# A two-layer graph attention kernel: one aggregate of layer 0 divided once more, its left sums made in the two aggregates in front

## The chip, the cores and the metric

The kernel runs on one core of a Trainium2 chip. The metric is the device time in microseconds of one execution. The kernel before was timed three times: 3044.36, 3051.23 and 3053.49 us, median 3051.23 us.

Engines are named as in the profile: PE is TensorE (PEld its weight loads), DVE is VectorE, ACT is ScalarE, POOL is GpSimd, SP is the engine that issues most loads.

## The reference

Two attention layers over 2708 nodes with 1024 features each. In both, every node attends to its neighbours in `adj`; the kernel spends its time in float32 products of 1024- and 2708-sized matrices.

```python
# layer 0
h = jnp.maximum(_layernorm(x), 0.0)
f = h @ Wf + bf;  g = h @ Wg + bg
e = relu(f @ g.T)
attention = softmax(where(adj > 0, e, NEG), axis=1)
x = x + attention @ (h @ W + bW)
# layer 1
h = jnp.maximum(_layernorm(x), 0.0)
hw = h @ W1
e = leaky_relu(hw @ a1 + (hw @ a2).T, 0.2)
attention = softmax(where(adj > 0, e, NEG), axis=1)
x = x + relu(attention @ hw)
```

The kernel multiplies by W after the attention: `(attention @ h) @ W`. The product `attention @ h`, before its multiplication by W, is called the aggregate here.

## The kernel before

**Tiling.** Rows of the attention (the nodes that look) come in five panels of 576, 576, 532, 512 and 512. The nodes that are looked at come in twenty tiles of 128, as ten pairs (`NQ`, a "pair" is also called q), with a small rest in two more tiles, MONO and TINY, called the left-over. The exponentials of one panel stay in on-chip memory: two tiles for each pair, plus two for the left-over.

**Products with seven instead of eight multiplications.** Every large product is split in 2 x 2 blocks and computed by Winograd's variant of Strassen's method with the seven products M1 to M7. Some operands are blocks as they are, some are sums and differences of blocks. The sums of the left side are made once and kept in HBM; those of the right side (the exponentials) are made on VectorE in place.

- In layer 0 the left side of the aggregate is `hg_d`, five tensors, each for two pairs, with the seven operands of 512 columns. `rows_h` writes the four that are blocks, `sums_h` reads them back, makes the other three and overwrites M5.
- `aggregate` (line 914) computes one panel's aggregate with `accumulate` (line 657). A product is 10 pairs x 4 blocks of 128 output rows, 40 matmuls, whose moving side is half a panel wide: 256 columns in panels 3 and 4. The order is M1, M5, M2, M6, M3, M7, M4. The results are collected in the temporary tiles m1, m15, u2 and in the result tile `gT`.
- In layer 1 the same is done for panel 0. In panels 1 to 4 `aggregate_quartered` (line 1085) is used: each of the seven products is split once more in the same way. A product is then seven inner products of 5 x 2 matmuls with a quarter of a panel as moving side, 128 columns in panels 3 and 4. `quarters_of` (line 1028) makes the inner sums of the right side in tiles named `quarter`, five for each product, four sums in each. `put_quarters` makes those of the left side (tiles `hq`) from `hr_d` and stores them in `hs2_d`. An inner product loads one tile `hc2`; two tiles `hl2` per product hold the last part of it.

**Order of work.** All loads on SP run in the program's order. Work that isn't urgent is put in lists of items, each with an assumed cost in us: `later` and `lazy`. After groups of matmuls the program calls `behind(us)`, which gives so much credit and runs items while credit is left; `lazy` is only used when `later` is empty and `spare[0]` is set, which in layer 0 is during the aggregates of panels 1 to 4. Before an item runs, the loads of the first `ahead[0]` items of its list are issued. `accumulate` calls `behind(rate)` four times in each product, with a rate of 3.0 in layer 0's aggregates; `aggregate_quartered` calls `behind(fine)` after each inner product. Beyond this, instructions without a fixed order are placed by a scheduler when the program is built, by when their inputs and buffers should be free.

**Around the change.** For every panel p layer 0 runs scores, the q-projection of the next panel (in which the softmax steps of this panel begin), the aggregate, and then, for panels 0 to 2, the projection by W. Panel 3's projection comes after the scores of panel 4, so the aggregate of panel 3 lies between a q-projection and scores. Layer 1's left sums `put_quarters` enter `lazy` as soon as four tiles of layer 0's result are known.

**Buffers.** `slot` has 54 buffers for panel-wide tiles, `stream` (tag "strm") 12 buffers of 4 KB per partition for tiles that are loaded and used once.

Of the kernel before, what the change touches and what calls it, by code (L numbers as in the profile page):

```python
# [8 lines left out]
FP = mybir.dt.float32  # L9
# [9 lines left out]
P = 128  # L19
W = 512  # L20
# [37 lines left out]
def kernel(  # L58
# [94 lines left out]
    hs_d = [dram.tile([P, 8, NH, P], FP, name=f"hs_d{q}") for q in range(NQ)]  # L153
    groups = [[q, q + 1] for q in range(0, NQ, 2)]
    group_of = {q: (i, j) for i, g in enumerate(groups) for j, q in enumerate(g)}
    assert sorted(group_of) == list(range(NQ))
    hg_d = [dram.tile([P, 7, len(g), W], FP, name=f"hg_d{i}") for i, g in enumerate(groups)]
    NK = NQ // 2
    WH = W // 2
    hr_d = dram.tile([P, 7, 2, 2, NK, WH], FP, name="hr_d")  # L160
    hs2_d = dram.tile([P, 7, 4, NK, WH], FP, name="hs2_d")

# [205 lines left out]
    def rows_h(q, ha, hb):  # L368

        i, j = group_of[q]  # L370
        for m, h in ((M1, ha[0]), (M5, ha[1]), (M2, hb[0]), (M4, hb[1])):
            store(hg_d[i][:, m, j], h)

    summed, sums_may = [0], [True]

    def sums_h():

        def fetch(q, two):
            i, j = group_of[q]
            for m in (M1, M2):  # L380
                two.append(stream("hr", (P, 2, W)))
                (load if "m" in got else by_scalar)(two[-1], hg_d[i][:, m:m + 2, j])

        def first(q, two):
            (a0, a1), (b0, b1) = ((t[:, 0], t[:, 1]) for t in two)
            add(b1, a1, b1)
            sub(a1, a0, a1)

        def second(q, two):
            (a0, a1), (b0, b1) = ((t[:, 0], t[:, 1]) for t in two)  # L390
            sub(a0, b1, a0)
            sub(b0, b0, a0)
            i, j = group_of[q]
            store(hg_d[i][:, M6:M7 + 1, j], two[0])
            store(hg_d[i][:, M3, j], b0)
            store(hg_d[i][:, M5, j], b1)
            summed[0] += 1
        for q in range(NQ):
            two = []
            put(1.4, lambda q=q, two=two: held(first, q, two), lambda q=q, two=two: fetch(q, two), ready=lambda: sums_may[0])  # L400
            put(1.4, lambda q=q, two=two: held(second, q, two), ready=lambda: sums_may[0])

    BY_QUARTERS = (M1, M5, M2, M6, M7, M3, M4)
    made_quarters = {}

    def put_quarters(m, k, to=lazy):

        two = []

        def fetch():  # L410
            if from_slots[0]:
                two.extend(slot(f"hq{h}", (P, 2, WH)) for h in range(2))
            else:
                t = stream("hq", (P, 4, WH))
                two.extend(t[:, 2 * h:2 * h + 2] for h in range(2))
            for h in range(2):
                nc.gpsimd.dma_start(two[h], hr_d[:, m, h, :, k])

        def go():
# [5 lines left out]
            for h in range(2):  # L425
                store(hs2_d[:, m, 2 * h:2 * h + 2, k], two[h])
            made_quarters[m] = made_quarters.get(m, 0) + 1
        put(1.7, go, fetch, to=to)

    def quarters_until(m):  # L430
        while made_quarters.get(m, 0) < NK:
            one(lazy if lazy else later)
# [491 lines left out]
    def aggregate(l, p, S, sm, then={}, rate=3.0):  # L924
# [28 lines left out]
        order_of_products = (M1, M2, M4, M5, M6, M3, M7) if first else (M1, M5, M2, M6, M3, M7, M4)  # L953
        steps = [(m, i) for m in order_of_products for i in range(len(groups))]

        def left(m, q, d):
            i, j = group_of[q]
            at = steps.index((m, i))
            for m_, i_ in steps[at:at + (3 if l else 1)]:
                if (m_, i_) not in hc:  # L960
                    hc[m_, i_] = stream("hc", (P, 4, WH) if l else (P, 2, W))
                    load(hc[m_, i_], hr_d[:, m_, :, :, i_].rearrange("p h f c -> p (h f) c") if l else hg_d[i_][:, m_])
            return hc[m, i][:, d // 2 * 2 + j, d % 2 * P:(d % 2 + 1) * P] if l else hc[m, i][:, j, d * P:(d + 1) * P]
# [70 lines left out]
    def quarters_of(p, S):  # L1034
# [47 lines left out]
        def fourth():  # L1082
            for q in range(NQ):
                sub(t1(q), wb_(q)[:, lo], wa_(q)[:, lo])
        return {"make": make, "right": right, "first": first, "fifth": fifth, "second": second, "fourth": fourth}

    def aggregate_quartered(p, S, sm, of_right, then={}, fine=1.2):

# [11 lines left out]
        def product(m, n, ps, start):  # L1100
            quarters_until(m)
            if (m, 0) not in lasts:
                for i, of in enumerate((hr_d[:, m, :, :, NK - 1].rearrange("p h f c -> p (h f) c"), hs2_d[:, m, :, NK - 1])):
                    lasts[m, i] = stream("hl2", (P, 4, WH))
                    load(lasts[m, i], of)
            t = stream("hc2", (P, NK - 1, WH))
            raw = n in (M1, M2, M4)
            i = {M1: 0, M2: 1, M4: 3, M6: 0, M3: 1, M7: 2, M5: 3}[n]
            load(t, hr_d[:, m, i // 2, i % 2, :NK - 1] if raw else hs2_d[:, m, i, :NK - 1])
            last = lasts[m, int(not raw)][:, i]  # L1110
# [10 lines left out]
        def left_over(banks, e, s, fresh):  # L1121

            two = stream("hl", (P, W + 2 * P))
            load(two, hgl_d[1][:, e])
            cols = lambda b: slice(s.start + b * hb, s.start + (b + 1) * hb)
# [43 lines left out]
        def with_second():  # L1169
# [3 lines left out]
        before_next = {M1: lambda: make(M5), M5: with_second, M2: lambda: (of_right["fourth"](), make(M6)), M6: lambda: make(M7),  # L1173
                       M7: lambda: make(M3), M3: lambda: make(M4)}
        left_out = None
        for m in BY_QUARTERS:
            V = [quad(*direct[m])[:, 2 * r:2 * r + 2] for r in range(2)] if m in direct else [v[:, :, :h] for v in in_pairs("V")]
            c11, c12 = (V[0][:, :, b * hb:(b + 1) * hb] for b in range(2))
# [39 lines left out]
            if m == M5:  # L1218
                of_right["second"]()
            if m == M5:  # L1220
                inverse.append(inverse_sums(p, sm))
            if m in then:
# [356 lines left out]
    def rows_done(t, xt):  # L1579
# [14 lines left out]
        if panel_of[t] == NP - 1:  # L1594
# [18 lines left out]
            else:  # L1613
# [16 lines left out]
                if q == NQ - 1:  # L1630
                    for m in BY_QUARTERS:
                        put_quarters(m, q // 2, later)
                    for p in range(2, NP):
# [16 lines left out]
        elif whole:  # L1650
# [3 lines left out]
            if quads_met[q // 2] == 2:  # L1654
                put(0.0, lambda: [put_quarters(m, q // 2) for m in BY_QUARTERS])

# [10 lines left out]

    ORDERED = (NP - 1,)

    def by_gpsimd(o, i, **k):  # L1670
# [97 lines left out]
    for p in range(NP):  # L1768
# [20 lines left out]
        spare[0], from_slots[0] = p > 0, p == NP - 1  # L1789
        G[p] = aggregate(0, p, S, got["sm"], then)  # L1790
        spare[0] = False
        if p == 0:
            flush()
            ahead[0] = 2
# [113 lines left out]
    for p in range(NP):  # L1908
# [5 lines left out]
        ahead[0] = 2 if p else 4  # L1914
        g = aggregate_quartered(p, S, sm, next_right, then, fine=1.0) if p else aggregate(1, p, S, sm, then, rate=4.0)
        hooks = {}
# [33 lines left out]
```

## Time and profile before

| | |
|---|---|
| three timed executions | 3044.36, 3051.23, 3053.49 us |
| the profiled execution | 3049.19 us |
| its span, first to last instruction | 3047.3 us |
| mean granted TensorE clock | 0.997 |
| HBM read / written | 630.04 MB / 138.11 MB |
| layer 0, aggregate of panel 1 | 838.8 to 987 us |
| layer 0, aggregate of panel 2 | 1235.8 to 1373 us |
| layer 0, aggregate of panel 3 | 1610.4 to 1742.4 us |
| layer 0, aggregate of panel 4 | 1926 to 2056.6 us |
| layer 1, aggregate of panel 3 (split) | 2698.3 to 2823.3 us |

How to read it: a busy share is a share of the span. A float32 matmul counts as two instructions on PE. Tile names in the trace are without their numbers, so `hs2_d` appears as `hs_d`, `hc2` as `hc` and `hl2` as `hl`; stages are told apart by their times. A chain of waits follows the work back from the last instruction, at each step to what released it.

### The profile page before, as it was taken

Reading aid. Unit: us, or ns where it says so; the run is one execution under the profiler, and the core shown is the slowest. Engines: PE = TensorE matmul, PEld = TensorE weight load, DVE = VectorE, ACT = ScalarE, POOL = GpSimd, SP = SyncE. Lnnn points to the kernel's source line nnn. Section 1 sums busy time; section 2 is a strip of 40 time slices with the busy share of each in tenths; the row PEclk is TensorE's granted clock in tenths of the full one; section 3 lists DMA queues with packets and bytes.
Section 4 is the critical chain, followed back from the end, with each engine's and each line's share of the span. In section 5 each row is a group of like instructions: output and inputs, shape, how many; then the busy total and the mean of one; then the engine's idle time right before and its main releaser. Section 6 shows DMA issues by size and latency. Waiting matters only on the chain.

```text
span 3047.3 us, 41722 instructions
## 1 busy us (share of the span) xinstructions
PE 2993.9 (98%) x14642; PEld 2294.2 (75%) x14642; DVE 2047.6 (67%) x4667; ACT 536.8 (18%) x880; POOL 496.9 (16%) x770
## 2 busy tenths in 40 slices
PE   8998999999999999999999999999999999999999
PEld 4576777667877588885888886784767959879695
DVE  5776794585742686616965276867878768887863
ACT  4420020020200121101210111302232121212200
POOL 1421111210112110223111111131212010020201
PEclk9999999999999999999999999999999999999999
DMA  6989878887466786768957588679768768878887
GB/s 232 302 271 272 311 276 308 264 286 235 133 236 165 228 273 195 247 156 251 292 188 251 179 241 258 223 292 335 245 212 264 263 202 299 294 265 297 264 294 268
DMA packets 392704, 766.78 MB, mean 252 GB/s; under 512 B 65728, under 2 KB 206944, under 8 KB 392464
## 3 DMA queue, kind: packets, MB, share of 16 engines
q1 hardware_dynamic: 332336, 584.80, 59.6%
q0 software_dynamic: 54464, 164.78, 16.1%
q10 hardware_dynamic: 5696, 14.55, 1.4%
q8 instruction: 116, 1.90, 0.2%
q14 instruction: 92, 0.75, 0.1%
HBM read 630.04 MB, written 138.11 MB: 252 GB/s over the span
## 4 chain that ended last, share of the span: by engine, by line
PE 73%; DVE 11%; issue 8%; DMA 5%; POOL 1%; ACT 1%; SPq 1%; POOLq 0%; DVEq 0%; ACTq 0%
PE sz L1425 6%; PE gy L679 6%; PE gz L679 6%; PE gz L1114 5%; PE gx L679 5%; PE sx L1425 4%; PE pz L1314 4%; PE sy L1425 4%; PE px L1314 4%; PE py L1314 3%; PE gy L1114 3%; PE gx L1114 3%; PE gv L679 3%; PE M_ps L591 3%; PE qz L679 2%
## 5 line engine op out<-in xcount | busy, mean ns | idle before, releaser
L1425 PE MATMUL sz<-B,As 128*128 128x288 f32 (+2 forms) x1200 | 292.0, 392 | 6.0 <-DVE st L45 5.1
L1425 PEld LDWEIGHTS sz<-B,As 128*128 128x128 f32 x1200 | 227.2, 190 | 55.2 <-DVE st L45 8.4
L1425 PE MATMUL sx<-B,As 128*128 128x288 f32 (+2 forms) x800 | 200.8, 394 | 12.4 <-DMA As<-hs_d 10.4
L1425 PE MATMUL sy<-B,As 128*128 128x288 f32 (+2 forms) x800 | 199.0, 392 | 0.0
L1425 PEld LDWEIGHTS sx<-B,As 128*128 128x128 f32 x800 | 152.5, 191 | 45.8 <-DMA As<-hs_d 9.5
L679 PE MATMUL gz<-Sa,hc 128*128 128x288 f32 (+2 forms) x800 | 185.8, 392 | 0.0
L679 PEld LDWEIGHTS gz<-Sa,hc 128*128 128x128 f32 x800 | 151.5, 190 | 32.2 <-issue 2.2
L1425 PEld LDWEIGHTS sy<-B,As 128*128 128x128 f32 x800 | 151.7, 190 | 30.6 <-DVE st L45 0.3
L1114 PE MATMUL gz<-quarter,hc 128*128 128x128 f32 (+2 forms) x1344 | 168.8, 279 | 3.8 <-DVE gT L45 3.7
L1114 PEld LDWEIGHTS gz<-quarter,hc 128*128 128x128 f32 x1344 | 160.6, 191 | 5.1 <-DVE gT L45 4.6
L143 POOL DMA_DIRECT2D out_dram<-x_res x164 | 81.2, 502 | 469.1 <-DVE x_res L45 461.9
L1314 PE MATMUL py<-w,ps 128*128 128x512 f32 x320 | 142.0, 593 | 0.0
L1314 PE MATMUL pz<-w,ps 128*128 128x512 f32 x320 | 142.0, 594 | 0.0
L1314 PE MATMUL px<-w,gT 128*128 128x512 f32 x320 | 141.1, 593 | 0.0
L679 PE MATMUL gy<-T,hc 128*128 128x288 f32 (+2 forms) x480 | 114.9, 402 | 3.8 <-DMA hc<-hg_d 3.8
L1314 PEld LDWEIGHTS pz<-w,ps 128*128 128x128 f32 x320 | 60.2, 190 | 76.2 <-issue 72.2
L1314 PEld LDWEIGHTS py<-w,ps 128*128 128x128 f32 x320 | 60.5, 190 | 75.1 <-issue 72.7
L591 PE MATMUL M_ps<-wgT,wfT 128*128 128x512 f32 x256 | 112.7, 596 | 1.6 <-ACT hsT L45 1.6
L1314 PEld LDWEIGHTS px<-w,gT 128*128 128x128 f32 x320 | 60.1, 190 | 71.3 <-issue 67.8
L679 PEld LDWEIGHTS gy<-T,hc 128*128 128x128 f32 x480 | 93.1, 194 | 24.7 <-DMA hc<-hg_d 4.3
L143 POOL DMA_DIRECT2D mk_d<-mask x55 | 35.9, 654 | 456.4 <-DVE mask L45 439.4
L45 ACT ACTIVATE P<-P 128x576 f32<-128x576 f32 (+3 forms) x111 | 72.1, 650 | 207.3 <-DVE P L45 207.2
(391 smaller groups left out, 5819.6 us busy)
## 6 DMA issues: line engine op xcount, KB each, us to landing
hc<-hg_d SPq DMA_DIRECT2D x175, 512.0 KB
As<-hs_d SPq DMA_DIRECT2D x150, 512.0 KB
hc<-hr_d SPq DMA_DIRECT2D x119, 512.0 KB
hc<-hs_d SPq DMA_DIRECT2D x112, 512.0 KB
w<-wt_d SPq DMA_DIRECT2D x96, 512.0 KB
w<-in_L_gnn_W_dram SPq DMA_DIRECT2D x72, 512.0 KB
md<-md_d SPq DMA_DIRECT2D x56, 512.0 KB
adj_i<-in_adj_dram SPq DMA_DIRECT2D x200, 128.0 KB
```

The lines of the kernel that those rows point to most:

```text
L45: i = f(*a, **k)
L143: nc.gpsimd.dma_start(a, b)
L591: nc.tensor.matmul(ps, wfT[a][c // NH][:, c % NH, :], wgT[b][c], start=(c == 0), stop=(c == NC - 1))
L679: nc.tensor.matmul(ps[d], left(m, k, d), right(m, k), start=(start and k == 0), stop=(k == K - 1), skip_group_check=True)
L1114: nc.tensor.matmul(ps[:, d], lhs[:, d * P:(d + 1) * P], inner_right(m, n, k), start=(start and k == 0 and d == 0), stop=(k == NK - 1), ski ...
L1314: nc.tensor.matmul(ps, left[i][m][:, k, :], w_[k], start=(start and k == 0), stop=(k == NH - 1), skip_group_check=True)
L1425: nc.tensor.matmul(ps[:n, :h], lefts[q][:, i % 2, c, :n], B[m][c // 2][:, c % 2, :h], start=(start and c == 0), stop=(c == NH - 1), skip_g ...
```

## The change

The aggregate of layer 0's panel 3 (`SPLIT_EARLY = (3,)`) is computed by `aggregate_quartered`, which now takes the layer as its first argument. In layer 0 its first two products, M1 and M5, stay whole and run through `accumulate`; the other five, M2, M6, M7, M3 and M4, are split in seven inner products each.

- The left sums of these five products (5 products x 5 parts = 25 items) are put in `lazy` after the aggregate of panel 0, each with an assumed cost of 5.5 us (layer 1's have 1.7). An item loads 512 KB on POOL, makes four sums on VectorE and stores 512 KB in two pieces.
- `hg_d` becomes one tensor whose parts of two pairs lie behind each other; `hs2_d` gets one tensor for each layer.
- The right side's inner sums for M2 are made in the middle of M5 (`with_second`).
- The collecting tiles V of this aggregate come from the stream buffers, and the result of M1 is written to two places of `gT`.
- Unsplit blocks are loaded from `hg_d` in pieces of half a row of a pair.

```diff
+    hg_d = dram.tile([P, 7, NK, 2, W], FP, name="hg_d")
-    hs2_d = dram.tile([P, 7, 4, NK, WH], FP, name="hs2_d")
+    hs2_d = [dram.tile([P, 7, 4, NK, WH], FP, name=f"hs2_d{l}") for l in range(2)]
...
-    BY_QUARTERS = (M1, M5, M2, M6, M7, M3, M4)
+    BY_QUARTERS = ((M2, M6, M7, M3, M4), (M1, M5, M2, M6, M7, M3, M4))
...
-    def put_quarters(m, k, to=lazy):
+    def put_quarters(l, m, k, to=lazy):
         two = []
         def fetch():
+            if l == 0:
+                t = stream("hq", (P, 2, 2, WH))
+                nc.gpsimd.dma_start(t.rearrange("p f h c -> p f (h c)"), hg_d[:, m, k])
+                two.extend(t[:, :, h] for h in range(2))
+                return
...
-        put(1.7, go, fetch, to=to)
+        put(1.7 if l else 5.5, go, fetch, to=to)
...
         def product(m, n, ps, start):
-            quarters_until(m)
+            quarters_until(l, m)
             if (m, 0) not in lasts:
+                rows = hr_d[:, m, :, :, NK - 1] if l else hg_d[:, m, NK - 1].rearrange("p f (h c) -> p h f c", h=2)
...
             t = stream("hc2", (P, NK - 1, WH))
...
+            load(t, hs2_d[l][:, m, i, :NK - 1] if not raw else hr_d[:, m, i // 2, i % 2, :NK - 1] if l else
+                 hg_d[:, m, :NK - 1, i % 2, i // 2 * WH:(i // 2 + 1) * WH])
...
+        def collected():
+            if l == 0:
+                t = stream("V", (P, NH, h))
+                return [t[:, 2 * r:2 * r + 2, :h] for r in range(2)]
+            return [v[:, :, :h] for v in in_pairs("V")]
+
+        if l == 0:
+            hc = {}
+            def left(m, q, d):
+                i, j = q // 2, q % 2
+                if (m, i) not in hc:
+                    hc[m, i] = stream("hc", (P, 2, W))
+                    load(hc[m, i], hg_d[:, m, i])
+                return hc[m, i][:, j, d * P:(d + 1) * P]
+            def first_product(d, ps):
+                nc.scalar.copy(quad(0, lo)[:, d], ps)
+                nc.scalar.copy(quad(1, lo)[:, d], ps)
+            exps_until(NQ)
+            of_right["fifth"]()
+            accumulate(left, of_right["operand"], NQ, h, (M1, M5), then,
+                       {M1: first_product, M5: lambda d, ps: add(quad(0, hi)[:, d], ps, quad(0, lo)[:, d])}, "g",
+                       {M5: sums_of_columns}, rate=rate, by_k=True, more={(M5, NQ // 2): with_second})
...
-        for m in BY_QUARTERS:
+        for m in BY_QUARTERS[l]:
...
+    SPLIT_EARLY = (3,)
...
-        G[p] = aggregate(0, p, S, got["sm"], then)
+        if p in SPLIT_EARLY:
+            G[p] = aggregate_quartered(0, p, S, got["sm"], quarters_of(p, S), then)
+        else:
+            G[p] = aggregate(0, p, S, got["sm"], then)
         spare[0] = False
         if p == 0:
+            for m in BY_QUARTERS[0]:
+                for k in range(NK):
+                    put_quarters(0, m, k)
             flush()
```

## The prediction

> **What bounds the kernel now.** First the page's busy shares and the chain of work that ended last, to see which engine sets the end.
>
> ```profile
> span 3047.3 us, 41722 instructions
> PE 2993.9 (98%) x14642; PEld 2294.2 (75%) x14642; DVE 2047.6 (67%) x4667; ACT 536.8 (18%) x880; POOL 496.9 (16%) x770
> PE 73%; DVE 11%; issue 8%; DMA 5%; POOL 1%; ACT 1%; SPq 1%; POOLq 0%; DVEq 0%; ACTq 0%
> ```
>
> TensorE has work 98% of the time; only what shortens its queue, or makes it wait, moves the end. Next the same busy times by stage: layer 0's aggregates of panels 1, 2 and 3, and layer 1's aggregate of panel 3, which is already split in the way that is now wanted and has the same width of 512.
>
> ```profile
> 838.80:987.00 148.20, 148.20 (x630) 114.24 (x629) 47.80 (x110) 6.05 (x13) 27.82 (x28) 1.00 0.67 200
> 1235.80:1373.00 137.20, 137.20 (x630) 114.24 (x629) 45.14 (x110) 4.66 (x11) 29.70 (x34) 1.00 0.69 208
> 1610.40:1742.40 132.00, 132.00 (x630) 114.16 (x629) 47.31 (x118) 11.14 (x16) 20.42 (x21) 1.00 0.72 223
> 2698.30:2823.30 125.00, 122.70 (x1126) 121.21 (x1125) 100.26 (x282) 22.89 (x43) 4.57 (x10) 1.00 0.88 301
> ```
>
> The columns are length, then busy PE, PEld, DVE, ACT and POOL, granted clock, DMA share, GB/s. The three layer 0 stages hold no idle TensorE at all, VectorE is a third busy, and the transfers have room. The split stage in layer 1 is shorter, but its transfers run at 0.88 and TensorE stands 2.3 us. The chain of waits gives the price of a product in both forms.
>
> ```profile
> 1610.55 17.27 PE gx L679 x80
> 1627.82 17.27 PE gy L679 x80
> ...
> 2715.55 4.47 PE gz L1114 x40
> ...
> 2888.58 4.47 PE gz L1114 x40
> ```
>
> A whole product is 40 matmuls, each two instructions: 80 in 17.27 us, 215.9 ns apiece. In the split form 40 instructions take 4.47 us, 111.75 ns apiece. Last, the left sums ("hq", now only layer 1's), by VectorE's timeline of panel 2's aggregate and VectorE's waits in panel 4's.
>
> ```profile
> 1245.55 8.46 DVE L45 TENSOR_TENSOR hq<-hq 128x256 f32<-128x256 f32 x25
> ```
> ```profile
> DVE hq L45 <- DMA hq<-hr_d: 5.8, 4, 2.7
> ```
>
> One sum costs 0.34 us when they follow each other; and VectorE, which works in order, can be held by a late load of them.
>
> **What the Trainium skill says.** "TensorE: Matmul & The Clock Gate", section Back-to-back issue gap, has 134 cycles at 128 columns against 262 at 256, a little over half; the trace agrees (111.75 against 215.9 ns). "Perfetto Trace Analysis", section Optimizing Scalar/DVE Operations, says that every VectorE instruction carries a fixed overhead, so small ones are dear; the trace agrees, with 281 ns for 128 columns, about 410 for 256 and 683 for 512. "DMA: Bandwidth & Descriptors", section Issuing engines are not separate DMA queues, says that transfers issued by SP and by POOL run on the same 16 engines: the new sums' transfers compete with TensorE's operands. Its section Where 436 GB/s comes from puts the limit of HBM at about 358 GB/s a core. The split stage moves 301 GB/s at a share of 0.88, which is 342 at full share; I use 342.
>
> **The change, part by part.**
>
> *The five products (gain).* Each was 80 instructions, 17.27 us; now 7 x 10 matmuls are 140 instructions of 111.75 ns, 15.65 us. Five times 1.62 is 8.1 us. The left-over rows go from 2.46 us (1713.08 to 1715.54) to 2.54 (2773.76 to 2776.30), four times: 0.3 back. Net 7.8 us of TensorE's queue, all of it on the path.
>
> *Waits inside the split products.* Layer 1's two such stages at this width lose 2.3 us (125.00 less 122.70) and 1.2 us. The first includes the start, which here is covered: the sums of M2 on the right side (20 subtractions, 4.5 us) are made in the middle of M5. Against this stands the shortage of buffers. "slot" has 54: 22 S, 14 B of the next panel, 5 T1, the sum and its inverse, 4 running maxima are 47. The old form added six; the new adds two sets of five quarter tiles, 57, and panel 4's first masks want three more. So the later quarters of the next product wait until the one before lets go. VectorE makes one k's four in 0.9 us and TensorE needs one each 0.45 us, with a left-over product of 2.2 us in front: 0 to 2 us for each of M6, M7, M3. Bounds for all waits 0 and 7 us; I take 2.5.
>
> *The 25 left sums in aggregates 1 and 2.* Each is a POOL load (512 KB), four VectorE sums and two POOL stores. 100 sums of 0.34 us are 34 us of VectorE in 285 us where it is busy 93: hidden. 75 POOL issues of 0.71 us are 54 us beside 57 busy: hidden, except where a store stands behind one that waits; POOL also gives the rows of the residual their bias at the end of panel 2's aggregate and waited 18.7 us there for these rows. The order: an aggregate calls `behind` 28 times with 3.0, 84 of credit; the last softmax steps take up to 5.6. At 5.5 apiece the first aggregate does 15, the second 10 and has some 23 left.
>
> *Layer 1's sums moved back.* They stand behind the 25 in the list. Before, 7 ran in each of the aggregates 1 and 2, at 1.7. Now 23/1.7 gives 13 or 14 of these 14 at the tail of aggregate 2, and 0 to 2 go over to aggregate 3, beside its own 7. Transfers: aggregate 1, 200 x 148.2 = 29.6 MB, less 7.3, plus 15 x 1.05: 38 MB, 257 GB/s. Aggregate 2, 28.5 less 7.3 plus 10.5 plus 13: 44.7 MB, 326 GB/s, near the 342, most of it in the tail where the weights and rows of the next projection are fetched too. TensorE's hc buffers run several ahead (ten loads issued within 26 us from 1235.03, against 3.6 us used per load), so I charge only the border to that projection: bounds 0 and 6 us, taken 1.5. The cover gone, it would be the last evictions behind VectorE's waits for hq.
>
> *Aggregate 3's transfers.* 10 hc loads (5.2 MB), 35 hc2 (18.4), 10 hl2 (5.2), 4 hl (1.6), adjacency and masks (2.1): 32.5 MB, and 1.05 for each of layer 1's sums. TensorE's new length is 132.0 - 7.8 = 124.2 us, in which 342 GB/s move 42.5 MB: up to 9.5 sums fit. With 7 to 9 it just does. SP issues the first As loads of panel 4's scores behind more loads: 0.5 us, bounds 0 and 2.
>
> *With one answer.* The joined `hg_d` tensor: layer 1's `hr_d` is one tensor as well, and its loads at 2089.16 ran while stores to other parts (2087.01, 2091.84) were on their way, so no new wait. Loads of V into stream buffers instead of slots, second copies of M1 on ScalarE (0.37 us each, busy 11 of 132): nothing.
>
> Sum: -7.8 + 2.5 + 1.5 + 0.5 = -3.3 us against the profiled execution's 3049.2, so 3045.9. The median of the three times, 3051.2, is 2.0 above that execution: 3048 for the median.
>
> **Rivals.**
> - *Clean*: no new waits, -7.8, 3043. For it: three stages without any idle TensorE and a third of VectorE used. Against: both split stages in layer 1 show waits.
> - *Cancelled*: quarter buffers and the border to the projection cost their upper ends (7 + 2 to 6), about +2, 3053. For it: 57 buffers wanted of 54. Against: quarters come free one by one, as fast as they are made.
> - *Transfers bind (slower)*: the `later` list takes more credit than the softmax's 5.6, so layer 1's sums are left for aggregate 3, where the bytes rise most. Beyond 9.5 sums each costs 1.05 MB at 342 GB/s, 3.07 us; VectorE then waits in order for hq, and the evictions behind it. From 14 sums on it is slower by more than 0.3%; at 16 it gives 6.5 x 3.07 = 20 us more, 3068; taken 3065. For it: 326 GB/s in the stage in front, and 0.88 in the model. Against: the credit counted above, and that hq can lag without TensorE.
> - *It doesn't do what it says*: sums not made in time are forced in front of the product that needs them, in a row, 1.6 us or more each. Part of the last rival; the credit speaks against it.
>
> **How the numbers follow.** Forecast 0.42, clean 0.12, cancelled 0.16, transfers 0.30. About 0.3%, 9 us, can be told from no change here (3042 to 3060). Even the clean case stays inside it, so faster has only half of that case and a little of the forecast's lower end: 0.10. Slower is nearly all of the transfers' case and a part of the cancelled one: 0.33. The same: 0.57. The forecast's own range is 3043 to 3053; with the bounds above (-7.8 and up to +15 less 7.8) and the rival, 3041 to 3066.
>
> **What would show it.** In the windows: panel 3's aggregate near 127 us with PE busy about 124; instructions on L1114's successor of 111.75 ns; aggregates 1 and 2 at 148 and 137 us still without idle TensorE, at about 257 and 326 GB/s; hq sums from 850 us on spread to 1373. Wrong would be: PE waits for hc in the five products, VectorE's waits for hq in tens of us, layer 1's hq sums running after M2 of aggregate 3 in number, or a shift elsewhere as large as these, since a new order of the buffers can move waits in stages that the diff doesn't touch.

## The result, and the profile after

The change made the kernel slower: 3088.84 us median (3074.46 to 3095.64, four runs) against 3050.55 us (3044.36 to 3053.49, four runs) before; ratio 1.0124, 95% interval 1.0101 to 1.0147, so the loss of 1.2% is clear of the spread. The profiled execution has a span of 3093.9 us, 46.6 more than before.

The page's head after the change (span, busy times, chain of waits by engine; the shares of this chain add to only 58%, so the chain is read below in one stretch alone):

```profile
span 3093.9 us, 42935 instructions
PE 2998.3 (97%) x15006; PEld 2305.8 (75%) x15006; DVE 2130.4 (69%) x4896; ACT 539.9 (17%) x890; POOL 538.8 (17%) x843
PE 42%; DVE 8%; DMA 4%; issue 2%; POOL 1%; ACT 1%; SPq 0%; POOLq 0%; DVEq 0%; ACTq 0%
```

TensorE is busy 4.4 us more than before although the products shrank; the other 42 of the 46.6 us are idle time. Line numbers such as L679 are those of the kernel that was profiled: in the kernel before, `accumulate` begins at line 665, `aggregate` at 924, `quarters_of` at 1034 and `aggregate_quartered` at 1087. Layer 0's aggregates of panels 1, 2 and 3 by windows (length, then busy PE, PEld, DVE, ACT, POOL, granted clock, DMA share, GB/s):

```profile
838.80:993.00 154.20, 150.33 (x630) 115.31 (x629) 65.78 (x147) 6.06 (x13) 44.13 (x55) 0.99 0.75 245
1241.60:1414.50 172.90, 141.69 (x630) 116.87 (x629) 73.75 (x173) 4.78 (x11) 69.25 (x90) 0.91 0.76 253
1659.20:1783.90 124.70, 124.19 (x993) 118.83 (x993) 82.71 (x245) 9.54 (x22) 13.35 (x19) 1.00 0.93 310
```

The changed stage itself, the third line, is 7.3 us shorter (132.00 before) and TensorE hardly stands in it. The two stages in front, whose products were not touched, are 6.0 and 35.7 us longer. Panel 2's projection adds some 8 us; these four make about 42 of the 46.6, and the rest lies in later stages by 1 to 3 us each. What TensorE waited for in panel 2's aggregate, from its list of waits there (us in total, times, longest):

```profile
PE sum_ps L903 <- DVE gT L45: 25.9, 1, 25.9
PE gv L679 <- DVE m L45: 5.3, 1, 5.3
```

Both are evictions that VectorE made late: the additions that carry a product's result into the tiles gT and m, without which TensorE can't go on. (In panel 1's aggregate the same wait is 3.9 us.) VectorE's timeline in the same stretch says why (start, length, operation, and in brackets the idle time before it and what ended it):

```profile
1353.26 1.80 DVE L45 TENSOR_TENSOR hq<-hq 128x256 f32<-128x256 f32 x4 [7.69 <-DMA hq<-hr_d]
1355.62 1.81 DVE L45 TENSOR_TENSOR hq<-hq 128x256 f32<-128x256 f32 x4 [0.57 <-DMA hq<-hr_d]
1360.44 1.81 DVE L45 TENSOR_TENSOR hq<-hq 128x256 f32<-128x256 f32 x4 [3.01 <-DMA hq<-hr_d]
1362.17 1.45 DVE L45 TENSOR_TENSOR gT<-gy,u 128x266 f32<-128x266 f32 x4
...
1389.01 1.81 DVE L45 TENSOR_TENSOR hq<-hq 128x256 f32<-128x256 f32 x4 [8.01 <-DMA hq<-hr_d]
1390.73 1.45 DVE L45 TENSOR_TENSOR m<-gw,m 128x266 f32<-128x266 f32 x4
```

The evictions (`gT<-gy,u`, `m<-gw,m`) start the moment a group of four left sums ends, and that group had waited for its load. VectorE stands idle in front of it with the eviction behind: from 1240 to 1400 us it waits 57.5 us for layer 1's loads of `hq` and 21.9 for layer 0's. It isn't busy, and the transfers aren't at their limit either, in the stretch in which layer 1's 14 items run (columns as above):

```profile
1305.50:1391.00 85.50, 54.50 (x244) 44.35 (x242) 34.12 (x69) 0.00 (x0) 44.57 (x56) 0.85 0.71 245
```

That the loads come one at a time is seen on POOL, which issues stores and loads of the same items (L143 stores, L408 loads of layer 0's items):

```profile
1281.45 0.57 POOL L408 DMA_DIRECT2D hq<-hg_d  x1
1287.94 0.71 POOL L143 DMA_DIRECT2D hs_d<-hq  x1 [5.92 <-DVE hq L45]
1288.87 0.72 POOL L143 DMA_DIRECT2D hs_d<-hq  x1 [0.22 <-issue]
1289.59 0.57 POOL L408 DMA_DIRECT2D hq<-hg_d  x1
1296.24 0.71 POOL L143 DMA_DIRECT2D hs_d<-hq  x1 [6.08 <-DVE hq L45]
```

From one load's issue to the next are 8.1 us: the load lands, VectorE makes four sums in 1.8, and POOL, waiting to issue the stores of this item, can't issue the next load. The chain of waits after the change goes through the same pieces (start, length, what):

```profile
1289.59 5.22 DMA hq<-hg_d
...
1296.24 7.95 DMA hs_d<-hq
1304.19 1.31 issue
1305.50 0.73 POOL hq L417
1306.23 3.18 DMA hq<-hr_d
```

The Trainium skill, "DMA: Bandwidth & Descriptors", section Anatomy of one DMA, gives each transfer a fixed part of about 2 us beside its bytes. The trace has 5.22 us for 512 KB, of which the bytes at the prediction's 342 GB/s would be 1.5 (an estimate); that a small part of it is the bytes agrees, but the two together make 3.5 and the trace is longer. What the rest is isn't shown. An item that runs alone pays such a latency for its load each time, and when the program counted credit (5.5 us for an item of layer 0, 1.7 for one of layer 1) it was not in the 1.7: layer 1's 14 items in this stage took from 1305.5 to 1391, 6.1 us each.

Slow items do a second thing. In the lines above the load at 1305.50 is issued only after a store of 7.95 us has landed, and SP, which loads TensorE's rows, waits in the same way. TensorE's rows and the items' tiles share the twelve buffers of `stream`, and an item's store is the last to use the item's buffer. SP's own waits for these stores, in panel 2's aggregate of the kernel before and of the changed one:

```profile
SPq L139 <- DMA hs_d<-hq: 13.9, 8, 2.2
SPq L139 <- DMA hs_d<-hq: 83.6, 17, 12.4
```

TensorE's rows were loaded far enough ahead to bear this; the projection's weights came 5.0 us late.

### The profile page after: what moved, and what is told of

Read it like the earlier page. It is cut to its first block, busy times and chain, and to the rows that moved or that the text cites. A ratio compares the mean times of both kernels' runs of the same rounds, so it can differ in the third digit from the quotient of the medians.

```text
span 3093.9 us, 42935 instructions
## 1 busy us (share of the span) xinstructions
PE 2998.3 (97%) x15006; PEld 2305.8 (75%) x15006; DVE 2130.4 (69%) x4896; ACT 539.9 (17%) x890; POOL 538.8 (17%) x843
## 4 chain that ended last, share of the span: by engine, by line
PE 42%; DVE 8%; DMA 4%; issue 2%; POOL 1%; ACT 1%; SPq 0%; POOLq 0%; DVEq 0%; ACTq 0%
PE gz L1120 6%; PE gx L1120 4%; PE gy L1120 4%; PE gx L679 3%; PE gy L679 3%; PE pz L1347 3%; PE py L1347 3%; PE px L1347 3%; PE sz L1458 2%; PE gz L679 2%; DVE P L45 2%; PE sx L1458 2%; PE sy L1458 2%; DMA hq<-hr_d 1%; DVE quarter L45 1%
## 5 line engine op out<-in xcount | busy, mean ns | idle before, releaser
L1120 PE MATMUL gz<-quarter,hc 128*128 128x128 f32 (+2 forms) x1584 | 198.2, 278 | 3.8 <-DVE gT L45 3.7
L45 DVE TENSOR_TENSOR hq<-hq 128x256 f32<-128x256 f32 x212 | 92.4, 461 | 157.4 <-DMA hq<-hg_d 85.6
L1120 PEld LDWEIGHTS gz<-quarter,hc 128*128 128x128 f32 x1584 | 188.6, 191 | 5.2 <-DVE gT L45 4.6
L143 POOL DMA_DIRECT2D out_dram<-x_res x164 | 81.0, 500 | 469.5 <-DVE x_res L45 458.1
L679 PE MATMUL gz<-Sa,hc 128*128 128x288 f32 (+2 forms) x640 | 152.3, 398 | 0.0
L679 PEld LDWEIGHTS gz<-Sa,hc 128*128 128x128 f32 x640 | 122.6, 192 | 28.6 <-issue 1.8
L143 POOL DMA_DIRECT2D mk_d<-mask x55 | 35.8, 651 | 540.7 <-DVE mask L45 426.2
L679 PE MATMUL gy<-T,hc 128*128 128x288 f32 (+2 forms) x480 | 111.9, 394 | 3.7 <-DMA hc<-hg_d 3.7
L143 POOL DMA_DIRECT2D hs_d<-hq x120 | 86.2, 721 | 162.8 <-DVE hq L45 153.6
```

The lines of the kernel that those rows point to most:

```text
L45: i = f(*a, **k)
L143: nc.gpsimd.dma_start(a, b)
L679: nc.tensor.matmul(ps[d], left(m, k, d), right(m, k), start=(start and k == 0), stop=(k == K - 1), skip_group_check=True)
L1120: nc.tensor.matmul(ps[:, d], lhs[:, d * P:(d + 1) * P], inner_right(m, n, k), start=(start and k == 0 and d == 0), stop=(k == NK - 1), ski ...
```

## The experiments

All ratios are to runs of the kernel before on the same chip. An item is one load, four sums and two stores. The lengths of the stages, read from TensorE's timeline to about 1 us, with the number of items that VectorE summed in each in parentheses:

| kernel | L0 panel 1 | L0 panel 2 | L0 panel 3 | L0 panel 4 | L1 panel 0 |
|---|---|---|---|---|---|
| before | 148 (7) | 137 (7) | 132 (7) | 131 (7) | 152 (7) |
| after | 154 (16) | 173 (23) | 125 (7) | 133 (7) | 152 (7) |
| e1_l1_held | 149 (16) | 137 (9) | 171 (21) | 130 (7) | 151 (7) |
| e13_seven_each | 148 (16) | 137 (9) | 126 (7) | 130 (14), then 25 idle | 164 (14) |
| e14_seven_stay | 150 (16) | 149 (16) | 125 (7) | 130 (7) | 160 (14) |
| e18_stay_act | 148 (16) | 137 (16) | 124 (7) | 130 (7) | 162 (14) |
| e19_three_places | 149 (16) | 143 (19) | 130 (9) | 134 (7) | 153 (9) |

### The parts alone

**e3_split_only**: the 25 items of layer 0 left out; the split products read unsummed rows of the same size, so the result lacks these sums.

```diff
-                    put_quarters(0, m, k)
+                    pass
```


> Layer 0's 25 left sums are left out altogether and the split products read unsummed rows of the same size instead; all else is as in the changed kernel. This prices the split alone: by the sum of the prediction and the wait of 0.5 us seen in panel 3's aggregate 7 us under the kernel before, 3043 us, whatever holds the sums up. If the split moved waits into other stages, 3050 us or more.

3043.26 us (before 3048.99), ratio 0.9978 [0.9971, 0.9985]. The five products gain what was predicted of them: panel 3's aggregate takes 124.0 us, 8.0 less than before, and TensorE never stands. The whole gains only 5.7, since panel 4's aggregate (133 us against 131) and layer 1's panel 1 (139 against 137) are longer by 2 us each; why is not shown.

```profile
1609.90:1733.90 124.00, 124.00 (x993) 118.80 (x993) 82.76 (x245) 9.48 (x22) 13.39 (x19) 1.00 0.93 307
```

**e4_sums_only**: the reverse; the sums made, nothing split.

```diff
-    SPLIT_EARLY = (3,)
+    SPLIT_EARLY = ()
```


> Panel 3's aggregate is whole again as before, while the 25 left sums are still made (nothing reads them). If the sums are the whole loss and the split the gain, the time is the changed kernel's plus 7 us: 3090 to 3100 us, with the same long waits in panel 2's aggregate. If part of the loss came from the split stage, it lies nearer to 3051 us.

3094.45 us, ratio 1.0148 [1.0123, 1.0173], with `sum_ps` waiting 27.7 us for `gT`. The whole loss comes with the sums.

**e2_no_sums**: VectorE's additions taken away from layer 0's 25 and layer 1's first 14 items; loads and stores stay, so what is stored is unsummed.

```diff
+            if l == 1 and k > 1:
                 add(a22, a21, a22)
...
```


> The four VectorE sums are left out of layer 0's 25 items and of layer 1's fourteen for the panels 0 and 1; their loads and stores stay (what is stored is what was loaded). If VectorE waiting in order for these loads is the cause, TensorE no longer waits for evictions behind them: 3042 to 3052 us, with the waits of 25.9 and 5.3 us gone. If the transfers are the cause, all of them are still made: 3080 to 3090 us.

3065.58 us, ratio 1.0055 [1.0037, 1.0073]. The waits for evictions go, and another takes their place: TensorE waits for the projection's weights, because SP's loads in order stand behind rows that had no stream buffer. From TensorE's waits, SP's waits and SP's timeline:

```profile
PE py L1348 <- DMA w<-wt_d: 19.8, 1, 19.8
SPq L139 <- DMA hs_d<-hq: 83.5, 13, 17.0
```
```profile
1314.95 37.73 SPq L139 DMA_DIRECT2D hc<-hg_d  x6
...
1361.39 3.17 SPq L139 DMA_DIRECT2D w<-in_L_gnn_W_dram  x4
```

The time lies between the two that were expected. Measured from e3, about half of the loss is gone (ratio 1.0055 against 1.0124, where e3 has 0.9978). This does not divide the loss between VectorE's order and the buffers: without additions the stores have nothing to wait for on VectorE, and the wait for weights may have been hidden behind the other one.

### Where the displaced sums go

**e1_l1_held**: layer 1's 14 items kept back until panel 3's aggregate.

```diff
+        put(1.7 if l else 5.5, go, fetch, to=back if l and to is lazy and not l1_may[0] else to)
...
+        if p == 3:
+            l1_may[0] = True
+            lazy.extend(back)
```


> Layer 1's fourteen left sums of the panels 0 and 1 are kept back until panel 3's aggregate begins; layer 0's 25 stay. If VectorE is held in order by layer 1's sums at the tail of panel 2's aggregate (25.9 + 5.3 us of TensorE's waits there), these waits go and the time falls by some 35 to 40 us, to 3045 to 3055 us. If the bytes of the added sums are what costs, they only move to panel 3's aggregate, which then passes the 9.5 sums that fit by 11.5, at 3.07 us each: the time stays at 3080 to 3090 us. If layer 0's own 25 sums are at fault, nothing changes: 3089 us.

3089.72 us, ratio 1.0130 [1.0107, 1.0153], in the range expected if the cost only moves. The aggregates of panels 1 and 2 are clean, with all 25 items of layer 0 in them; the loss has moved whole to panel 3's. Its waits, and a window of it:

```profile
PE gx L1122 <- DMA hc<-hg_d: 25.2, 4, 9.6
PE gz L1122 <- DMA hc<-hs_d: 4.5, 1, 4.5
```
```profile
1232.60:1369.70 137.10, 137.10 (x630) 114.21 (x629) 47.82 (x117) 4.63 (x11) 34.45 (x41) 1.00 0.70 224
1643.00:1720.00 77.00, 43.12 (x298) 41.15 (x297) 41.71 (x119) 1.49 (x4) 33.33 (x47) 0.77 0.97 330
```

There the transfers do bind, at a share of 0.97 and 330 GB/s, with 21 items, where the prediction put the point at 9.5 and the rate at 342. Layer 0's items cost next to nothing as long as no others stand behind them in the same aggregate.

**e8_l1_first**: layer 1's items in front of layer 0's in the list.

```diff
+        if l and to is lazy:
+            lazy.insert(front[0], lazy.pop())
+            front[0] += 1
```


> Layer 1's sums enter the lazy list in front of layer 0's, at their old charge of 1.7: in each aggregate first the seven that the kernel before ran there too, at the start, where their loads can be issued during the q-projection; then layer 0's at 5.5. By credit 12 or 13 of layer 0's fit in each of the two aggregates. If the loss is only that layer 1's sums were pushed to the end of panel 2's aggregate, none of its waits is left and the split's gain shows: 3042 to 3048 us. If 32 items in two aggregates are too many in any order, it stays above 3060 us.

3082.0 us, ratio 1.0115 [1.0098, 1.0132]; the theory that only the order is at fault fell. Panel 1's aggregate takes 166 us with 21 items, panel 2's 157 with 18. Now it is layer 0's items that stand late in front of the same eviction (VectorE's timeline):

```profile
1362.88 1.80 DVE L45 TENSOR_TENSOR hq<-hq 128x256 f32<-128x256 f32 x4 [11.61 <-DMA hq<-hg_d]
1364.60 1.45 DVE L45 TENSOR_TENSOR gT<-gy,u 128x266 f32<-128x266 f32 x4
```

So it is not whose sums come last that counts, but that there are too many in an aggregate.

**e5_cost55**: layer 1's items charged 5.5 us too.

```diff
-        put(1.7 if l else 5.5, go, fetch, to=to)
+        put(1.7 if l and to is later else 5.5, go, fetch, to=to)
```


> Layer 1's left sums are charged 5.5 instead of 1.7 while they stand in the lazy list, as layer 0's are; nothing else. If what costs is that 14 of them are packed into the tail of panel 2's aggregate, faster than one load-sum-store can follow another there (some 5.8 us each), then about 5 are left there at a pace of some 8 us and the waits of 25.9 and 5.3 us shrink to 5 or less; about 9 go over to panel 3's aggregate, at the same slow pace: 3050 to 3062 us. If any sum of layer 1 behind layer 0's costs the same, wherever it runs: 3085 us or more.

3102.8 us, ratio 1.0185 [1.0167, 1.0204], in the second of the two ranges expected: the higher charge leaves 15 items in panel 2's aggregate, which takes 152 us, and carries others on, so that panel 3's has 12 (6.9 us of waits for `hc<-hg_d` there); 17.8 us of waits for `gT` are left. The low charge by itself is not the cause.

### What makes an item slow

**e6_load_by_act**: the items' loads issued by ScalarE, so that they don't stand behind stores on POOL. **e7_ahead4**: four items looked ahead in place of two. **e10_act_ahead4**: both.

```diff
-                nc.gpsimd.dma_start(t.rearrange("p f h c -> p f (h c)"), hg_d[:, m, k])
+                nc.scalar.dma_start(t.rearrange("p f h c -> p f (h c)"), hg_d[:, m, k])
...
-                nc.gpsimd.dma_start(two[h], hr_d[:, m, h, :, k])
+                (nc.scalar if k < 2 else nc.gpsimd).dma_start(two[h], hr_d[:, m, h, :, k])
...
-        ahead[0] = 1 if p == 0 else 2
+        ahead[0] = 1 if p == 0 else 4 if p < 3 else 2
```


> The loads of layer 0's items, and of layer 1's for the panels 0 and 1, are issued by ScalarE instead of POOL; stores stay on POOL. On POOL a load stands behind the stores of the item before, which wait for VectorE's sums. If this order sets the pace of an item, it is gone and the time falls below 3065 us. If the wait for a free stream buffer sets it, a load comes no sooner: 3080 to 3095 us.

> In the aggregates of panels 1 and 2 the loads of the first four items of a list are issued instead of two. If too short a lookahead is what holds VectorE, its waits for hq shrink and the time falls to 3050 to 3065 us. If buffers are what is short, the longer lookahead takes them from TensorE's operands and gains nothing, 3080 us or more, with new waits of TensorE for hc.

> Both edits that were tried alone, the items' loads issued by ScalarE and four items looked ahead in the aggregates of panels 1 and 2. Theory (an item takes 6 to 8 us because its load is issued behind the stores of the one before, and only loads that are issued earlier shorten it): with both, items overlap, the waits for gT fall below 10 us together, and the time goes to 3045-3062. Rival (the twelve stream buffers are the limit: more items ahead only hold buffers that the matmuls' own rows need): 3068-3085, with more time in waits of TensorE for hc or w.

3070.48 us, ratio 1.0075 [1.0049, 1.0100]; 3079.37, 1.0109 [1.0094, 1.0124]; 3062.68, 1.0050 [1.0032, 1.0069]. TensorE's waits in panel 2's aggregate and the border behind it, with both edits:

```profile
PE sum_ps L903 <- DVE gT L45: 11.9, 2, 6.6
PE py L1347 <- DMA w<-wt_d: 4.1, 1, 4.1
```

With both edits over half of the loss is gone, with ScalarE alone about two fifths: panel 2's aggregate has 23 items as in the changed kernel and takes 155 us in place of 173. Lookahead alone does little; on POOL the loads still stand behind the stores, and no new waits for `hc` appear, so the shortage that was its rival isn't seen. e6 lies between its two ranges and e10 just outside the lower one: its last item began at 1354, not early enough. That ScalarE's loads are simply quicker is not the reason. From issue to the first sum e6 has 6.0 us (1257.42 to 1263.42), the changed kernel 5.1 (1281.45 to 1286.54). The loads are issued sooner: layer 1's first one 56 us into the aggregate (1291.4) in place of 64 (1305.5).

**e9_sums_by_pool**: the additions issued to GpSimd. The edit took all items of the list `lazy`, 25 and 28, not 25 and 14 as its expectation says.

```diff
+            on = nc.gpsimd if to is lazy else nc.vector
+            for o, x, y, f in ((a22, a21, a22, OP.add), (a21, a11, a21, OP.subtract), (a11, a22, a11, OP.subtract), (a12, a12, a11, OP.subtract)):
+                on.tensor_tensor(o, x, y, f)
```


> The four additions of each item that is made in layer 0's spare credit (25 of layer 0, 14 of layer 1) are issued to GpSimd in place of VectorE; layer 1's last seven stay on VectorE. Theory (VectorE works in order, so evictions of panel 2's aggregate stand behind additions that wait for their loads): no wait of TensorE for gT of 16 us or more is left in that aggregate, and the time falls to 3042-3062; a part of the loss may come back as late stores or late loads. Rival (what is dear is that loads and stores stand one behind another, on whatever engine the additions are): the items get slower still with GpSimd's additions, the program waits for rows before panel 3's products, and the time stays at 3080 or more.

3147.56 us, ratio 1.0330 [1.0313, 1.0346]. The theory's first half holds and its number fails, while the time lies in the rival's range: no wait for `gT` is left in that aggregate, but the items are slower still and hold buffers (SP waits 165.7 us for their stores from 1240 to 1460), so the rows for TensorE are late. Behind the aggregates the weights are late too, by 13.0 us in panel 1's projection and 23.8 in panel 2's.

```profile
PE gz L678 <- DMA hc<-hg_d: 13.2, 1, 13.2
PE gv L678 <- DMA hc<-hg_d: 8.3, 2, 4.6
PE gv L970 <- DMA hl<-hgl_d: 6.3, 1, 6.3
```

### How many items an aggregate takes

**e11_l1_panel4** and **e12_l1_in_layer1**: e1's edit with the release at layer 0's panel 4, or at layer 1's panel 0. Panel 2's seven items (and panel 3's in the second) were kept back with them, as the edit holds all of layer 1's list until then: e11 has no item in panel 3's aggregate, 14 in panel 4's and directly behind it, and 21 in layer 1's panel 0; e12 has 29 of the 35 in layer 1's panel 0 and six in its panel 1.

> Layer 1's 14 items that are made in spare credit are kept back until panel 4's aggregate of layer 0. Theory (layer 0's 25 items cost next to nothing while nothing is queued behind them; what cost is where layer 1's go): the aggregates of panels 1, 2 and 3 of layer 0 show under 4 us of waits of TensorE for evictions or rows together, so that up to the end of panel 3's aggregate the span stands 5 to 8 us ahead of the kernel before; panel 4's aggregate then takes 21 items where it had seven, and gives 0 to 40 us back: 3042-3085 in all. Rival (layer 0's items are dear by themselves): 15 us or more of waits remain in the aggregates of panels 1 and 2.

> Layer 1's 14 items are kept back until the aggregate of layer 1's own panel 0, which needs none of them. Theory: as in the run before up to layer 0's end, and then 14 items in an aggregate of whole rows whose transfers and VectorE have room (its loads of three items ahead): 3041-3055, the version that may be faster than the kernel before. Rival (there is no room there either, VectorE is busy with exponentials of the next panel): waits of TensorE for evictions or rows of 15 us or more in that aggregate, 3058-3090.

3101.65 us, ratio 1.0178 [1.0160, 1.0195], and 3091.06 us, 1.0146 [1.0129, 1.0163]. Both are even with the split alone up to the end of panel 3's aggregate (1734 and 1731 us; 1742 before), which shows that layer 0's 25 sums are nearly free while none of layer 1 share their aggregates. Then e11 loses 24.0 us in front of panel 4's projection (`py` for VectorE's `ps`) and e12 25.3 at the end of layer 1's panel 0 (`sum_ps` for `gT`): above e11's range, and just above the rival's of e12.

**e13_seven_each**: of the 14, seven to panel 4 and seven to layer 1's panel 0. **e14_seven_stay**: seven stay in panel 2's aggregate, seven go to layer 1's panel 0.

```diff
+    kept_for = {0: 4, 1: 5}
...
+        put(1.7 if l else 5.5, go, fetch, to=kept[kept_for[k]] if l and to is lazy and k in kept_for else to)
```
(e14: `kept_for = {1: 5}`)

> Of layer 1's 14 items, seven (row group 0) are kept back until layer 0's panel 4 and seven (row group 1) until layer 1's panel 0, so that each of these aggregates takes 14 items where the two runs before gave one of them 21. Theory (an aggregate has room for some 14 to 25 items, and the wait comes only from those beyond it): no wait of TensorE for gT, ps or hc of 8 us or more from layer 0's panel 1 on, and 3040-3056: the gain of the five products comes out, faster than the kernel before if 3043 or less. Rival (in these two aggregates VectorE, with exponentials of the next panel, has no room for any added item): the waits come back in both, each some two thirds of what 21 items cost, and the time is 3065-3090.

> Row group 0's seven items of layer 1 stay where the changed kernel has them, behind layer 0's items in panel 2's aggregate; row group 1's seven are kept back until layer 1's panel 0. Theory (room by number: panel 2's aggregate then takes nine of layer 0 and seven of layer 1, at 8 and 6 us each some 115 of its 137 us): it shows less than 6 us of waits for evictions, and the whole is 3042-3065, what is lost being lost in layer 1's panel 0. Rival (any item of layer 1 behind layer 0's is too late for the last evictions): 10 us or more of waits in panel 2's aggregate, and 3065 or more.

3081.8 us, ratio 1.0108 [1.0091, 1.0125], and 3065.61 us, 1.0050 [1.0034, 1.0066]. e13's waits from panel 4 to layer 1's first projection:

```profile
PE py L1350 <- DVE ps L45: 24.7, 1, 24.7
PE sum_ps L906 <- DVE gT L45: 12.0, 1, 12.0
```

Panel 4 has no room: its softmax steps come first in the list, in the kernel before its own seven items ran from 2028 in an aggregate that ends at 2057. In e13 they begin at 2020, the aggregate ends at 2048, and most of the seven more stand in front of the projection's sums. Panel 2's aggregate takes nine items without loss and 16 with a wait of 9.9 us (with 23 the waits were 31.2). Both runs have the time of their rival and not of their theory.

### The best placing

**e17_stay_act_ahead** and **e18_stay_act**: e14 with the remaining loads by ScalarE, the first with four items ahead as well. **e19_three_places**: e18 with the seven dealt three, two and two.

```diff
+    kept_for = {(M6, 1): 3, (M7, 1): 3, (M3, 1): 5, (M4, 1): 5}
```


> Row group 1's seven items of layer 1 in layer 1's panel 0 as in the run before, and the loads of all items that stay in panels 1 and 2 issued by ScalarE, four items ahead. Theory (panel 2's aggregate still waited 9.9 us because its items came one at a time; with loads issued earlier its 14 items end by about 1320, some 50 us ahead of the last evictions): no wait for gT of 3 us or more in panels 1 and 2, and 3040-3054. Rival (the rest of that run's 18 us over the kernel with the five products alone is not in waits that panel 2's order causes): 3056-3068.

> As the run beside it, with two items ahead, as in the changed kernel. Theory: one item of the 16 in panel 2's aggregate takes about 5.2 us in place of 5.8, the items end by about 1330, and the wait for gT there is under 5 us: 3042-3058. If only the two edits together end the wait, this stays at 3058-3066 while the other falls.

> As the run with seven items of layer 1 kept back and loads by ScalarE, but the seven (row group 1) are dealt to three places by the room that the runs have shown: M1, M5 and M2 stay in panel 2's aggregate (19 items), M6 and M7 go to panel 3's (nine), M3 and M4 to layer 1's panel 0 (nine). Theory (amount per aggregate decides, at about 4.8 us an item in panel 2): panel 2's items end by about 1335, under 4 us of new waits in all, and layer 1's panel 0 takes about 154 us where 14 items made it 162: 3041-3050, level with the kernel before or a little faster. Rival (the last of the gain is taken by each added item wherever it stands): 3051-3058.

3060.99 us, ratio 1.0030 [1.0019, 1.0040]; 3053.87 us, 1.0020 [1.0013, 1.0028]; 3057.77 us, 1.0028 [1.0018, 1.0038]. e18 meets its range; e17 and e19 lie in their rivals'. The intervals of the three overlap, so which of them is best is not shown. In e17 the wait for `gT` did go, as its theory had it, but not the time: in its profile panel 1's aggregate begins at 841.6 us where e18's does at 835.6, a difference that arose ahead of the stages in question. In e18 panel 2's aggregate has no idle TensorE with the same 16 items; VectorE's last wait there is far ahead of the evictions (window, then timeline):

```profile
1232.60:1369.60 137.00, 137.00 (x629) 114.14 (x628) 59.11 (x145) 4.56 (x11) 41.00 (x49) 1.00 0.84 277
```
```profile
1317.54 1.80 DVE L45 TENSOR_TENSOR hq<-hq 128x256 f32<-128x256 f32 x4 [2.94 <-DMA hq<-hr_d]
1325.07 0.43 DVE L45 TENSOR_TENSOR gT<-gy,u 128x266 f32<-128x266 f32 x1 [5.73 <-PE gy L682]
```

At the last line VectorE waits for TensorE, as it should; in the changed kernel it was the other way round. 16 items took 78 us here and 95 in e14, 4.9 us each against 5.9, and the only edit between the two is the engine that issues the loads: the pace of the items sets how many fit. The rest of e18's loss is layer 1's panel 0, 162 us with 14 items where it had 152 with seven. e19 frees that stage (153) and pays in panels 2 and 3 (143 and 130 us). None of the versions that make all the sums is faster than the kernel before; whether some finer placing would be stays open.

## Why the prediction was wrong

It forecast 3048 us, no difference to be told, and the time is 3089, beyond its range (3041 to 3066). Step by step:

- *The five products, -7.8 us*: right. Panel 3's aggregate got 7.3 us shorter; the split without sums gained 5.7 us of the median (3048.99 to 3043.26).
- *Waits inside the split products, 2.5 us*: too high, and harmless. TensorE stood 0.5 us.
- *The credit count*: right. 15 and 10 items of layer 0 were forecast in the two aggregates, 16 and 9 ran; all 14 of layer 1 came at the tail of panel 2, and panel 3 kept its own seven. So the registered slower case, transfers binding from 9.5 sums on in panel 3, did not decide; e1 put 21 sums there and showed it at 0.97 and 330 GB/s. One sum is off: layer 1's 14 items are 14.7 MB at 1.05 each, not 13, which makes 338 GB/s in panel 2's aggregate. And 342 is no limit of the core, nor is the 358 that stands beside it: behind panel 4's aggregate the kernel before moves 415, 383 and 400 GB/s in three stretches of 12 us (2060 to 2096).
- *"I charge only the border to that projection: bounds 0 and 6 us, taken 1.5."* This is the step that failed. The border, the wait for weights, measured 5.0, inside its bounds. What came beside it, the late evictions, measured 25.9 and 5.3 us in panel 2 and 3.9 in panel 1. The prediction had named them ("the last evictions behind VectorE's waits for hq") as what comes when the cover is gone, and had priced them at nothing because it looked only at the bytes. The bytes were not the limit: while layer 1's 14 items ran, the transfers stood at a share of 0.71 and 245 GB/s. Latency was: items in series at 6 to 8 us, with VectorE waiting in order in front of an eviction. The sign that the prediction itself gave for being wrong, VectorE's waits for hq in tens of us, came with 79.4 us.
- *"34 us of VectorE in 285 us where it is busy 93: hidden"*: false in kind. 1.8 us of additions for each item are hidden, the wait in front of them is not, since VectorE can do nothing else in it. The same holds for POOL: its 0.71 us for an issue are small, but a store that waits for the sums holds the next load (5.92 and 6.08 us in the lines shown).
- *Before as the model*: 25 of the 28 sums of seven items in 8.46 us at 1245.55 gave the price of a sum. Those items had all their loads issued between 1207 and 1238 us, ahead of the aggregate or at its start; items behind a queue of 25 had not.
- *The scores' start, 0.5 us*: no such wait appeared.

What is shown: that the loss comes with the sums (e3, e4); that layer 0's are nearly free alone and the loss moves with layer 1's (e1, e11, e12), while putting layer 0's last instead doesn't help (e8); that it grows with the number of items in an aggregate (panel 2: 137 us with nine, 149 with 16, 173 with 23); and that loads issued sooner let more fit (e6, and e14 against e18). That TensorE's long waits came from VectorE standing in order is shown by the timeline, and by e2 and e9, in which they are gone. How the loss divides between this and the twelve stream buffers, which slow items hold, was not separated: in e2 and e9 waits for weights and rows came in its place.

## What to carry to other kernels

Work put into the idle time of an engine that works in order can cost its waits, not its busy time: count for each item the latency from its load's issue to the next item's load, multiply by the number of items, and compare with the time to the last urgent instruction on that engine. A trace in which such items ran back to back shows their price only if their loads will again be issued early. And when new background work enters a list, ask what it pushes back, and whether the place where that lands has room; here the new work was nearly free where it stood alone, and dear where the displaced work shared its stage. Count also how long each item holds a buffer that urgent loads need.

## What was unexpected of the hardware

- After a long stall TensorE also ran slower. In panel 2's aggregate the same 630 instructions took 141.69 us busy at a mean granted clock of 0.91, against 137.20 at 1.00 before; in e1's window of 77 us with TensorE busy 43, the clock was 0.77. So 4.5 us came on top of the 31.2 us of waits there. In the changed kernel TensorE stood from 1336.7 to 1362.7, and windows around this show the clock, the third figure from the end: it falls some us into the stall and is back some us after it.

```profile
1337.00:1340.00 3.00, 0.00 (x0) 0.00 (x0) 0.00 (x0) 0.00 (x0) 2.76 (x4) 1.00 0.86 285
1346.00:1362.00 16.00, 0.00 (x0) 0.00 (x0) 4.85 (x12) 0.00 (x0) 8.01 (x12) 0.50 0.85 297
1362.00:1366.00 4.00, 3.35 (x8) 2.68 (x9) 1.62 (x5) 0.00 (x0) 3.49 (x6) 0.53 0.92 321
1366.00:1370.00 4.00, 4.00 (x20) 3.38 (x19) 1.22 (x2) 0.00 (x0) 0.52 (x2) 1.00 0.76 273
```

  The lower clock follows the stall in time; that the stall is its cause was not tried by itself.
- GpSimd took 0.74 us (median) for an addition of 128x256 in e9 where VectorE takes 0.42 in the same run, so it was no free place for sums.
